# Two stacked row-and-column scans on one core: where the first pair's output and layer 1's residual are kept in DRAM, and when four groups of transfers are issued

## The chip, the cores and the metric

The kernel runs on one core of a Trainium2 chip. The time is device microseconds of the whole program on that core; the median of three runs is 4559.44 us.

## The reference, cut to what matters

`x` is (32, 48, 64, 128): batch, channel, height H, width W, all float32. Two layers run one after the other, and each adds four scans of the group-normalised input to its input. A scan step is a convolution of 5 taps over the 48 channels (width taps for the rows, height taps for the columns), with bias, plus the next line.

```python
def _conv1d(x, w, b):                      # 5 taps, padding 2
    y = jax.lax.conv_general_dilated(x, w, window_strides=(1,), padding=[(2, 2)], ...)
    return y + b[None, :, None]
def step(w, b):
    def f(carry, inp):
        nxt = inp + _conv1d(carry, w, b)
        return (nxt, nxt)
    return f
...
xs = jnp.moveaxis(x, 2, 0)
d0 = xs[0]
_, d_rest = jax.lax.scan(step(down_w, down_b), d0, xs[1:])     # down: rows 1..63
...                                                            # up: rows back to 0
_, r_rest = jax.lax.scan(step(right_w, right_b), r0, ws[1:])   # right: columns 1..127
...
_, l_rest = jax.lax.scan(step(left_w, left_b), l0, R[Ww - 2::-1])
...
x = x + _L0_conv_ref(_gn(x), L0_...)       # _gn: 16 groups of 3 channels, per image
x = x + _L1_conv_ref(_gn(x), L1_...)
return x
```

Every step needs the one before it, so the chain of steps is the spine of the program: 63 down, 63 up, 127 right and 127 left for each image and layer.

## The kernel before, in words

**Tiling.** The 32 images are four groups of 8 (`GB`). A row phase scans one group down and up: 126 steps. A column phase scans a pair of groups right and left: 254 steps. A step is nine products of 128x128 by 128 columns on TensorE (two instructions each) into three PSUM tiles, and three additions on VectorE (`step`, L630 to L657). The partitions hold (8 neighbouring rows or columns e) x (48 channels) in three tiles of 128 (`NG`, index o); `PIECES` lists the ten stretches of partitions that belong to one e, and every transfer that touches this layout is issued piece by piece.

**Phases.** `PHASES` is a fixed order of 12: rows of layer 0 groups 0 and 1, columns of layer 0 pair 0, rows 0/2, rows 1/0, rows 0/3, columns 0 pair 1, rows 1/1, 1/2, 1/3, columns 1 pair 0 (k = 10), columns 1 pair 1 (k = 11). Between a row phase and the column phase the data goes through DRAM (`ups`) to change layout; the input with rows in order is kept in `xin`, and layer 0's result, which layer 1 takes in, in `mid`. Both are lists of one DRAM tensor for each group (`kept`, `source`).

**Buffers.** SBUF has three slots. A row phase uses two of them. A column phase has four quarters of its columns and three slots: quarters 0 and 3 share one, so quarter 0 is written to DRAM (`spill_unit`) after the right scan has passed it and brought back before the left scan ends. A quarter has six units (o, group) of 128 x 2048 numbers, 1 MB. Four more 1 MB tiles (`stage`) hold residuals and results on their way; in layer 1 two are `nats` (residual in) and two are `perms` (result out).

**Output of a layer 1 column phase.** For each of 24 units, in the order of quarters 3, 2, 1, 0: `load_residual` on ScalarE's queue, `add_permuted` on GpSimd (eight additions that also reorder), and `store_result`, which writes runs of 32 numbers (128 bytes) into `out`, half on SyncE's queue and half on ScalarE's. Units of quarter 2 free the slot into which the next phase's quarter 0 is loaded, units of quarter 1 that for its quarter 1, and units of quarter 0 that for its quarter 2.

**Order.** Nothing is scheduled by the machine. `at(t, fn, ...)` puts a piece of work into `agenda` at a step number t; before each scan step the work due by then is emitted, and `in_order` ties each engine's instructions to that order. An engine's queue, SyncE's and ScalarE's DMA queues too, therefore runs strictly in this order, and each waits for what its next entry needs. The step number is a place in the order, not a time at which something is held back. `plan_rows` (L753), `plan_cols` (L790), `plan_input` (L733) and `first_group` (L912) fill the agenda.

**Places that the change touches.** `move_rows` (L500) moves rows between DRAM and the slots, in runs of 128 bytes. `plan_rows` stores the last rows of the up scan in the blocks 8 to 15, 2 to 7 and 0 to 1 when the column phase of the same pair follows (`follows`, true for k = 2 and k = 6). The column phase then loads quarter 0 of the second group in stretches on ScalarE's queue:

```python
at(t0 - 13 + i, load_unit, k, 0, i, 2, NH, 0, E8, other)     # rows 16 to 63
at(t0 - 6 + i / n, load_unit, k, 0, i, 1, 2, 0, E8, other)   # rows 8 to 15
at(t0 - 1.5, load_unit, k, 0, i, 0, 1, E8 // 4, E8, other)   # rows 2 to 7
at(t0, load_unit, k, 0, i, 0, 1, 0, E8 // 4, other)          # rows 0 and 1
```

In `first_group`, group 0 is loaded, permuted on GpSimd, written to `xin` and read back in the scan's layout by `move_rows`, then scaled on ScalarE by `scale_rows`; the last eight rows (56 to 63) are read back at step 20 of the agenda (L1040), behind the first loads of group 1 (`take_in`, L1036), and rows 48 to 63 are scaled at step 34 (L1042).

Of the kernel before, what the change touches and what calls it, by code (L numbers as in the profile page):

```python
# [30 lines left out]
C = 48  # L34
# [57 lines left out]
def kernel(  # L92
# [22 lines left out]
    NBN = H * W // (2 * BN)  # L115
    CHANNEL = H * W * GB
    PAD = 1024
    assert N == FULL and SLOT == NG * HALF * N and SLOT == 6 * UNIT

    cpool = ctx.enter_context(tc.tile_pool(name="cpool", bufs=1))  # L120
# [26 lines left out]
    def kept(name):  # L147

        return [
            dram.tile([C, CHANNEL + PAD], F32, tag=f"{name}{g}", name=f"{name}{g}")[:, 0:CHANNEL]  # L150
            for g in range(NGRP)
        ]

    source = [kept("xin"), kept("mid")]
    ups = [kept("upa"), kept("upb")]
    taps = [
        [dram.tile([C, TAPS, C], F32, tag=f"taps{i}{j}", name=f"taps{i}{j}") for j in range(3)]
# [3 lines left out]
        dram.tile([2 * NG, FULL, UNIT], F32, tag=f"spill{i}", name=f"spill{i}")  # L161
        for i in range(4)
    ]

    def by_row(t, e, h0, h1):


        t = t.rearrange("c (i q a e n) -> e a c i q n", i=E8, q=NQ, a=NH, e=E8)[e, h0 // E8]
        return t[:, h0 % E8 : h0 % E8 + h1 - h0].rearrange("c i q n -> c (i q) n")

    def lines(t, h0, h1):

        t = t.rearrange("c (i q a n) -> a c i q n", i=E8, q=NQ, a=NH)[h0 // E8]
        return t[:, h0 % E8 : h0 % E8 + h1 - h0].rearrange("c i q n -> c (i q) n")

    def by_col(t, e, j):


        return t.rearrange("c (i q n) -> i q c n", i=E8, q=NQ)[e, j]

    def dma(dst, src, queue=None):
        (queue or nc.sync).dma_start(dst, src)
# [21 lines left out]
    def pieces(o):  # L204
        return [(e, c0, c1, p0) for e, c0, c1, g, p0 in PIECES if g == o]
# [278 lines left out]
    def put_out(g, h, perm, stride):  # L484

        n = perm.shape[-1] // (W * GB)
        for s in range(2):
            dma(
                lines(source[0][g], h + s * stride, h + s * stride + n),
                perm[SIDES[s]].rearrange("p (m n) -> p m n", n=LINE),  # L490
            )

# [7 lines left out]
    def move_rows(k, h0, h1, to_dram):  # L500

        _, layer, g = PHASES[k]
        view = row_views(k)[h0 // HALF]
        t = (ups if to_dram else source)[layer][g]
        for h in range(h0, h1, E8):
            end = min(h1, h + E8)
            for o in range(NG):
                for e, c0, c1, p0 in pieces(o):
                    here = view[p0 : p0 + c1 - c0, o, h % HALF : h % HALF + end - h]
                    here = here.rearrange("p h (q n) -> p (h q) n", q=NQ)  # L510
                    there = by_row(t, e, h, end)[c0:c1]
                    if to_dram:
                        dma(there, here)
                    else:
                        dma(here, there)

    def scale_rows(k, h0, h1):
        _, layer, g = PHASES[k]
# [22 lines left out]
    def quarter(k, j):  # L541
        return slot[slots(k)[j % 3]].rearrange("p (o s n) -> p s o n", s=2, o=NG)
# [24 lines left out]

    HH = NH // 2  # L570

    def load_residual(k, j, i, nat):
        _, layer, pair = PHASES[k]
        if layer == 0:
            o, half = UNITS[i]
            t = source[0][2 * pair + half]
            for e, c0, c1, p0 in pieces(o):
                dma(nat[p0 : p0 + c1 - c0], by_col(t, e, j)[c0:c1])
            return
        o, r = divmod(i, 2)  # L580
        view = nat.rearrange("p (s n) -> p s n", s=2)
        part = slice(r * HH * LINE, (r + 1) * HH * LINE)
        for e, c0, c1, p0 in pieces(o):
            for s in range(2):
                dma(
                    view[p0 : p0 + c1 - c0, s],
                    by_col(source[1][2 * pair + s], e, j)[c0:c1, part],
                    nc.scalar,
                )

    def add_residual(k, j, i, nat):
        o, half = UNITS[i]
# [3 lines left out]
    def keep_result(k, j, i):  # L596
        _, layer, pair = PHASES[k]
        o, half = UNITS[i]
        for e, c0, c1, p0 in pieces(o):
            dma(  # L600
                by_col(source[1][2 * pair + half], e, j)[c0:c1],
                quarter(k, j)[p0 : p0 + c1 - c0, half, o],
            )

    def add_permuted(k, j, i, nat, perm, engines):
# [9 lines left out]
                    dst[:, a, s], res[:, a, s], inp[:, a, s], ALU.add  # L615
                )

    def store_result(k, j, i, perm):
        pair = PHASES[k][2]
        o, r = divmod(i, 2)  # L620
        both = out[2 * pair * GB : 2 * (pair + 1) * GB]
        dst = both.rearrange("b c (a e) w -> e a c b w", e=E8)[..., j * WQ : (j + 1) * WQ]
        src = perm.rearrange("p (a b n) -> p a b n", a=HH, b=2 * GB)
        for a in range(HH):
            for e, c0, c1, p0 in pieces(o):
                to = nc.sync if a < HH // 2 else nc.scalar
                dma(dst[e, r * HH + a, c0:c1], src[p0 : p0 + c1 - c0, a], to)


# [90 lines left out]
    def at(t, fn, *args):  # L720
        agenda.append((t, len(agenda), fn, args))
# [68 lines left out]
    def plan_cols(k, t0, prev):  # L790
        _, layer, pair = PHASES[k]
        n = 2 * NG
        after = prev == "cols"
        for i in range(n):
            if follows(k) and UNITS[i][1] == 1:
                other = nc.scalar
                at(t0 - 13 + i, load_unit, k, 0, i, 2, NH, 0, E8, other)
                at(t0 - 6 + i / n, load_unit, k, 0, i, 1, 2, 0, E8, other)
                at(t0 - 1.5, load_unit, k, 0, i, 0, 1, E8 // 4, E8, other)
                at(t0, load_unit, k, 0, i, 0, 1, 0, E8 // 4, other)  # L800
                at(t0 + 1.5, load_unit, k, 1, i)
            else:
                early = 30 if after else 46 if k == 2 else 70
                at(t0 - early + 2 * i, load_unit, k, 0, i)
                at(t0 + (3 if after else 0.5 if follows(k) else -24 + 2 * i), load_unit, k, 1, i)
            at(t0 + (38 if after else 8) + 2 * i, load_unit, k, 2, i)
            at(t0 + 33 + 2 * i, spill_unit, k, i, False)
            at(t0 + 50 + 2 * i, load_unit, k, 3, i)
        final = k == len(PHASES) - 1
        left = t0 + W - 1  # L810
        end = left + W - 1
        for i in range(n):
            at(left + 64 + 2 * i, spill_unit, k, i, True)
        units = []
        for n_done, j in enumerate((3, 2, 1, 0)):
            every = 4.5
            if j == 0 and PHASES[k + 1 if not final else k][0] == "rows":
                every = 7
            units += [(left + 34 + 32 * n_done + every * i, j, i) for i in range(n)]
        stats = None  # L820
        if layer == 0:
            stats = ResultStatsV(f"r{2 * pair}"), ResultStatsA(f"r{2 * pair + 1}")
        tiles = [stage[:, i] for i in range(4)]
        nats, perms = (tiles, None) if layer == 0 else (tiles[0:2], tiles[2:4])
        ahead = len(nats)

        for u, (t, j, i) in enumerate(units):
            nat = nats[u % ahead]
            o, half = UNITS[i]
            if u < ahead:  # L830
                at(left + 16, load_residual, k, j, i, nat)
            elif not (final and j == 0):
                at(units[u - ahead][0] + (3 if layer == 0 else 4.9), load_residual, k, j, i, nat)
            if layer == 0:
                at(t, add_residual, k, j, i, nat)
                at(t + 4, keep_result, k, j, i)
                unit = quarter(k, j)[:, half, o]
                if half == 0:
                    for b in range(GB):
                        at(t + 5 + b, stats[0].take, j, o, unit, b)  # L840
                else:
                    at(t + 1, stats[1].take, j, o, unit)
            elif not (final and j == 0):
                perm = perms[u % 2]
                at(t, add_permuted, k, j, i, nat, perm, [nc.gpsimd])
                at(t + 5, store_result, k, j, i, perm)
        if layer == 0:
            t = units[-1][0] + 14
            g = 2 * pair
            spread(t, scaling(f"r{g}", 1, g, stats[0], r_masks), 1)  # L850
            spread(t + 20, scaling(f"r{g + 1}", 1, g + 1, stats[1], r_masks), 1)
        if final:
            at(left + 97, last_loads, k)
            at(end + 4, last_results, k)
# [57 lines left out]
    def first_group():  # L912
# [119 lines left out]
        scale_rows(0, 24, 32)  # L1032
        move_rows(0, 32, 48, False)
        scale_rows(0, 32, 40)
        move_rows(0, 48, 56, False)
        take_in(1, 0, nats1[0])  # L1036

    in_order(first_group)
    at(starts[0] + 10, scale_rows, 0, 40, 48)
    at(starts[0] + 20, move_rows, 0, 56, 64, False)  # L1040
    at(starts[0] + 22, take_in, 1, 16, nats1[1])
    at(starts[0] + 34, scale_rows, 0, 48, 64)  # L1042

    agenda.sort(key=lambda a: a[:2])
    done = 0
# [65 lines left out]
```

## Time and profile before

| | |
|---|---|
| three runs | 4550.92, 4559.44, 4564.35 us |
| profiled execution | span 4546.3 us, mean granted TensorE clock 0.964 |
| TensorE busy | 4163.2 us, 92% of the span |
| DMA | 661.55 MB, mean 146 GB/s; 2010816 of 2124132 packets are under 512 bytes |
| chain that ended last | TensorE 77%, DMA 15% |

TensorE is the engine that matters: the scans are a chain. What can be won lies in the places where it stands still, before its first step, after its last, and between. The DMA row says that nearly all packets are small: `xin`, `ups` and `out` are reached in runs of 128 bytes when the layout changes, whereas quarters, spills and residuals move in runs of 4 or 8 KB. In the tables by stretch, the last two columns are the busy share of the 16 DMA engines and what they moved; a share of 1.0 or over is a stretch in which they are full.

### The profile page before, as it was taken

The numbers are of one execution on the slowest core, as the hardware profiler recorded it, in microseconds if no ns is written. First come the engines' busy times: TensorE is split into PE (matmuls) and PEld (weight loads), VectorE is DVE, ScalarE is ACT, GpSimd is POOL, SyncE is SP. The second block draws the span as 40 slices with busy tenths as digits, with TensorE's granted clock in tenths as the row PEclk, the third lists the DMA queues.
The fourth block names the chain that finished last, engine by engine and source line by source line (L and its number), as shares of the span: only waits on it lengthen the run. The fifth ranks groups of instructions, "written<-read, shape, count | busy, mean of one in ns | idle before, by whom it ended". The sixth has DMA issues, their size and how long they took to land.

```text
span 4546.3 us, 90798 instructions
## 1 busy us (share of the span) xinstructions
PE 4163.2 (92%) x36632; PEld 4132.1 (91%) x36632; DVE 2180.9 (48%) x6594; ACT 1183.5 (26%) x2334; POOL 907.7 (20%) x943
## 2 busy tenths in 40 slices
PE   4889997999999999979999999999999997879990
PEld 2889997999999999979999999999999997869990
DVE  5445443446654444434456654444444443334441
ACT  1553302426776445000025944330000000000000
POOL 4441001314412020000024300000000155500554
PEclk9999998999999999989999999999999998889995
DMA  9989789857989999489038989394790099970799
GB/s 176 176 163 157 114 146 194 202 105 237 221 163 160 162 150 155 75 151 199 6 89 241 204 148 150 48 143 84 117 207 12 18 195 181 200 188 1 148 172 163
DMA packets 2124132, 661.55 MB, mean 146 GB/s; under 512 B 2010816, under 2 KB 2063808, under 8 KB 2092224
## 3 DMA queue, kind: packets, MB, share of 16 engines
q1 hardware_dynamic: 1901312, 573.92, 66.5%
q10 hardware_dynamic: 222400, 81.83, 9.5%
q8 instruction: 288, 4.72, 0.5%
q14 instruction: 132, 1.08, 0.1%
HBM read 378.70 MB, written 277.11 MB: 144 GB/s over the span
## 4 chain that ended last, share of the span: by engine, by line
PE 77%; DMA 15%; SPq 2%; ACT 2%; POOL 1%; ACTq 1%; issue 1%; DVE 0%; POOLq 0%; DVEq 0%
DMA out<-arena 6%; PE step_01r L641 6%; PE step_00r L641 6%; PE step_10r L641 6%; PE step_00l L641 6%; PE step_01l L641 6%; DMA arena<-mid 4%; PE step_11r L641 3%; PE step_00u L641 3%; PE step_11d L641 3%; PE step_02u L641 3%; PE step_11u L641 3%; PE step_10u L641 3%; PE step_13u L641 3%; PE step_13d L641 3%; PE step_12u L641 3%
## 5 line engine op out<-in xcount | busy, mean ns | idle before, releaser
L525 ACT ACTIVATE arena<-arena,offset,scale 128x256 f32<-128x256 f32 (+2 forms) x840 | 594.7, 802 | 449.3 <-DVE arena L650 151.8
L614 POOL TENSOR_TENSOR arena<-arena 128x256 f32<-128x256 f32 x336 | 349.1, 1082 | 973.1 <-DVE arena L650 717.6
L482 POOL COPY arena<-arena 112x256 f32<-112x256 f32 x458 | 270.9, 648 | 764.1 <-DMA arena<-in_x 469.0
L880 ACT COPY arena<-arena 128x256 f32<-128x256 f32 x18 | 10.5, 644 | 1470.9 <-DMA out<-arena 1467.9
L594 POOL TENSOR_TENSOR arena<-arena 128x2048 f32<-128x2048 f32 x48 | 217.7, 4562 | 835.7 <-PE step_01l L641 543.5
L641 PE MATMUL step_11r<-arena,wright 128*128 128x128 f32 x2286 | 267.3, 281 | 85.7 <-DVE arena L650 37.6
L641 PEld LDWEIGHTS step_11r<-arena,wright 128*128 128x128 f32 x2286 | 265.4, 198 | 87.5 <-DVE arena L650 55.8
L416 ACT ACTIVATE junk<-arena 128x256 f32<-128x256 f32 x192 | 129.6, 675 | 699.2 <-POOL arena L594 693.1
L641 PE MATMUL step_01r<-arena,wright 128*128 128x128 f32 x2286 | 258.8, 277 | 29.3 <-DMA arena<-upa 29.3
L641 PEld LDWEIGHTS step_01r<-arena,wright 128*128 128x128 f32 x2286 | 258.4, 194 | 29.7 <-issue 29.5
L641 PE MATMUL step_00r<-arena,wright 128*128 128x128 f32 x2286 | 257.4, 276 | 29.2 <-DMA arena<-upa 29.2
L641 PEld LDWEIGHTS step_00r<-arena,wright 128*128 128x128 f32 x2286 | 257.0, 193 | 29.6 <-issue 29.4
L641 PE MATMUL step_00l<-arena,wleft 128*128 128x128 f32 x2286 | 256.3, 275 | 0.0
L641 PE MATMUL step_10r<-arena,wright 128*128 128x128 f32 x2286 | 256.0, 275 | 0.0
L641 PEld LDWEIGHTS step_10r<-arena,wright 128*128 128x128 f32 x2286 | 255.7, 192 | 0.3
L641 PEld LDWEIGHTS step_00l<-arena,wleft 128*128 128x128 f32 x2286 | 255.7, 192 | 0.0
L641 PE MATMUL step_01l<-arena,wleft 128*128 128x128 f32 x2286 | 255.4, 275 | 0.0
L641 PE MATMUL step_10l<-arena,wleft 128*128 128x128 f32 x2286 | 255.4, 275 | 0.0
L641 PE MATMUL step_11l<-arena,wleft 128*128 128x128 f32 x2286 | 255.4, 275 | 0.0
L641 PEld LDWEIGHTS step_01l<-arena,wleft 128*128 128x128 f32 x2286 | 255.3, 192 | 0.0
L641 PEld LDWEIGHTS step_10l<-arena,wleft 128*128 128x128 f32 x2286 | 255.3, 192 | 0.0
L641 PEld LDWEIGHTS step_11l<-arena,wleft 128*128 128x128 f32 x2286 | 255.3, 192 | 0.0
(173 smaller groups left out, 6989.0 us busy)
## 6 DMA issues: line engine op xcount, KB each, us to landing
xin<-arena SPq DMA_DIRECT2D x96, 384.0 KB, 5.5
arena<-xin SPq DMA_DIRECT2D x96, 384.0 KB, 8.5
mid<-arena SPq DMA_DIRECT2D x96, 384.0 KB, 8.0
arena<-mid SPq DMA_DIRECT2D x192, 192.0 KB, 4.4
upb<-arena SPq DMA_DIRECT2D x192, 192.0 KB, 3.9
arena<-mid ACTq DMA_DIRECT2D x192, 192.0 KB, 4.7
arena<-upb SPq DMA_DIRECT2D x96, 384.0 KB, 10.7
arena<-xin SPq DMA_DIRECT2D x186, 192.0 KB, 4.3
```

Of the source, the lines that this page charges most:

```text
L416: nc.scalar.activation(junk[:, 0:n], view[:, b], AF.Identity, accum_out=self.sum[:, i, j : j + 1])
L482: copy(dst[:, r, q], src[:, r0 + r, q])
L525: nc.scalar.activation(args[0], args[0], AF.Identity, bias=args[2], scale=args[1])
L594: nc.gpsimd.tensor_tensor(unit, unit, nat, ALU.add)
L614: engines[(2 * a + s) % len(engines)].tensor_tensor(dst[:, a, s], res[:, a, s], inp[:, a, s], ALU.add)
L641: nc.tensor.matmul(part(whole(ps[o]), -s), weights[:, i, FULL * (o - NG * s - i + 1) : FULL * (o - NG * s - i + 2)], part(src(i), s), star ...
L880: copy(dst[:, a, s], src[:, a, s])
```

## The change

1. `mid` becomes two tensors, one for each pair of groups, with the halves of a unit's rows (r) outside and the two groups (s) inside. So `load_residual` of layer 1 is one DMA of 8 KB runs for each piece in place of two of 4 KB runs, while `keep_result` (layer 0) writes 4 KB runs in place of 8 KB runs. `move_rows` of layer 1 reads the same 128-byte runs from other addresses.
2. In phase 10 the 12 units of quarters 1 and 0 are no longer stored into `out` from SBUF. Each is written as it stands, one DMA of 1 MB in 8 KB runs on SyncE's queue, into a DRAM tensor `held[n]`; later, behind all loads of phase 11's quarters in that queue's order, `store_result` moves it from `held[n]` into `out`, DRAM to DRAM, all on SyncE's queue.
3. At the two places where a column phase follows its own row phase, rows 32 to 63 of the second group's quarter 0 are loaded 18 steps earlier than rows 16 to 31.
4. In `first_group` rows 56 to 63 are read back with rows 48 to 55, ahead of the first loads of group 1, and rows 48 to 63 are scaled in two parts at steps 26 and 32 in place of one at step 34.

```diff
+    HH = NH // 2
-    source = [kept("xin"), kept("mid")]
+    xin = kept("xin")
+    mid = [
+        dram.tile([C, 2 * CHANNEL + PAD], F32, tag=f"mid{i}", name=f"mid{i}")[:, 0 : 2 * CHANNEL]
+        for i in range(NGRP // 2)
+    ]
...
+    held = [dram.tile([FULL, UNIT], F32, tag=f"held{i}", name=f"held{i}") for i in range(4 * NG)]
...
+    def pair_row(t, s, e, h0, h1):
+        t = t.rearrange("c (i q r s a e n) -> s r a e c i q n", i=E8, q=NQ, r=2, s=2, a=HH, e=E8)
+        r, a = divmod(h0 // E8, HH)
+        t = t[s, r, a, e][:, h0 % E8 : h0 % E8 + h1 - h0]
+        return t.rearrange("c i q n -> c (i q) n")
+    def pair_col(t, e, j):
+        return t.rearrange("c (i q r n) -> i q c r n", i=E8, q=NQ, r=2)[e, j]
...
         o, r = divmod(i, 2)
-        view = nat.rearrange("p (s n) -> p s n", s=2)
-        part = slice(r * HH * LINE, (r + 1) * HH * LINE)
         for e, c0, c1, p0 in pieces(o):
-            for s in range(2):
-                dma(
-                    view[p0 : p0 + c1 - c0, s],
-                    by_col(source[1][2 * pair + s], e, j)[c0:c1, part],
-                    nc.scalar,
-                )
+            dma(nat[p0 : p0 + c1 - c0], pair_col(mid[pair], e, j)[c0:c1, r], nc.scalar)
...
+            n = UNIT // 2
             dma(
-                by_col(source[1][2 * pair + half], e, j)[c0:c1],
-                quarter(k, j)[p0 : p0 + c1 - c0, half, o],
+                pair_col(mid[pair], e, j)[c0:c1, :, half * n : (half + 1) * n],
+                quarter(k, j)[p0 : p0 + c1 - c0, half, o].rearrange("p (r n) -> p r n", n=n),
             )
...
-    def store_result(k, j, i, perm):
+    def store_result(k, j, i, perm, queues=(nc.sync, nc.scalar)):
...
-                to = nc.sync if a < HH // 2 else nc.scalar
+                to = queues[a * len(queues) // HH]
...
-                at(t0 - 13 + i, load_unit, k, 0, i, 2, NH, 0, E8, other)
+                at(t0 - 31 + i, load_unit, k, 0, i, 4, NH, 0, E8, other)
+                at(t0 - 13 + i, load_unit, k, 0, i, 2, 4, 0, E8, other)
...
-                at(t + 5, store_result, k, j, i, perm)
+                if final or j > 1:
+                    at(t + 5, store_result, k, j, i, perm)
+                else:
+                    n = 2 * NG * (1 - j) + i
+                    at(t + 5, dma, held[n], perm)
+                    at(end + 104 + 4.5 * n, store_result, k, j, i, held[n], [nc.sync])
...
-        move_rows(0, 48, 56, False)
+        move_rows(0, 48, 64, False)
         take_in(1, 0, nats1[0])
...
-    at(starts[0] + 20, move_rows, 0, 56, 64, False)
     at(starts[0] + 22, take_in, 1, 16, nats1[1])
-    at(starts[0] + 34, scale_rows, 0, 48, 64)
+    at(starts[0] + 26, scale_rows, 0, 48, 56)
+    at(starts[0] + 32, scale_rows, 0, 56, 64)
```

More of the change, by code (lines that the diff above doesn't have):

```diff
@@ L488, in put_out @@
             dma(
-                lines(source[0][g], h + s * stride, h + s * stride + n),
+                lines(xin[g], h + s * stride, h + s * stride + n),
                 perm[SIDES[s]].rearrange("p (m n) -> p m n", n=LINE),
@@ L503, in move_rows @@
         view = row_views(k)[h0 // HALF]
-        t = (ups if to_dram else source)[layer][g]
+        t = ups[layer][g] if to_dram else mid[g // 2] if layer else xin[g]
         for h in range(h0, h1, E8):
@@ L510, in move_rows @@
                     here = here.rearrange("p h (q n) -> p (h q) n", q=NQ)
-                    there = by_row(t, e, h, end)[c0:c1]
                     if to_dram:
-                        dma(there, here)
+                        dma(by_row(t, e, h, end)[c0:c1], here)
+                    elif layer:
+                        dma(here, pair_row(t, g % 2, e, h, end)[c0:c1])
                     else:
-                        dma(here, there)
+                        dma(here, by_row(t, e, h, end)[c0:c1])
     def scale_rows(k, h0, h1):
@@ L566, in spill_unit @@
             dma(there, here)
-    HH = NH // 2
     def load_residual(k, j, i, nat):
@@ L575, in load_residual @@
             o, half = UNITS[i]
-            t = source[0][2 * pair + half]
+            t = xin[2 * pair + half]
             for e, c0, c1, p0 in pieces(o):
```

## The prediction

> **What bounds the kernel now.** I read the page first: TensorE is busy for 4163.2 of 4546.3 us, so at most some 380 us can be won, all of it where TensorE stands still. Next, who TensorE waited for (total, times, longest, in us):
>
> ```profile
> PE step_11r L641 <- DVE arena L650: 37.6, 4, 18.8
> PE step_00d L641 <- DVE arena L650: 34.8, 3, 19.2
> PE step_11r L641 <- DMA arena<-mid: 32.8, 2, 16.9
> PE step_01r L641 <- DMA arena<-upa: 29.3, 1, 29.3
> PE step_00r L641 <- DMA arena<-upa: 29.2, 1, 29.2
> PE step_11r L641 <- DMA arena<-upb: 15.3, 1, 15.3
> ```
>
> The three rows of step_11r are the start of phase 11: 85.7 us together. The two of about 29 us are the starts of phases 2 and 6, one 19.2 us stop of step_00d is phase 0. The names after the arrow are the last arrival, not the cause; the chain of waits gives that. For phase 11's last stop (start, length, what):
>
> ```profile
> 3977.87 12.26 DMA out<-arena
> ...
> 3991.21 7.51 DMA out<-arena
> ...
> 4017.48 9.53 DMA arena<-upb
> ...
> 4027.03 10.85 DMA arena<-upb
> ...
> 4038.41 1.65 PE step_11r L641 x6
> ```
>
> Phase 11's quarter 2 (upb) comes late because phase 10's output is late. Whether the DMA engines are full there, and at which rate, the table by stretch tells (span, TensorE, its loads, VectorE, ScalarE, GpSimd, clock, DMA share and GB/s):
>
> ```profile
> 400.00:450.00 50.00, 47.66 (x424) 47.30 (x423) 22.29 (x70) 23.22 (x31) 0.00 (x0) 1.00 1.01 157
> 1100.00:1150.00 50.00, 50.00 (x450) 50.00 (x450) 34.02 (x94) 39.75 (x99) 20.69 (x5) 1.00 1.01 299
> 3800.00:3840.00 40.00, 16.01 (x137) 15.53 (x135) 7.08 (x23) 0.00 (x0) 17.11 (x17) 0.73 1.10 178
> 3980.00:4000.00 20.00, 20.00 (x182) 20.00 (x181) 9.49 (x31) 0.00 (x0) 0.00 (x0) 1.00 0.98 265
> 4060.00:4220.00 160.00, 160.00 (x1434) 159.93 (x1433) 76.53 (x239) 0.00 (x0) 0.00 (x0) 1.00 0.02 5
> 4230.00:4426.00 196.00, 192.43 (x1724) 192.24 (x1722) 94.38 (x289) 0.00 (x0) 116.01 (x112) 1.00 0.92 180
> 4426.00:4546.00 120.00, 0.00 (x0) 0.00 (x0) 20.84 (x17) 10.47 (x18) 49.36 (x50) 0.50 1.03 164
> ```
>
> The first row is row moves in 128-byte runs alone: full at 157 GB/s. Runs of 8 KB reach 299 (loads) and 265 (loads beside spills). The stops of phase 11 lie in a full stretch at a mixed 178; 160 us of empty DMA follow at once; then phase 11's own output fills the engines to the end, 120 us past the last step. So a unit of 1 MB (1.049 million bytes) costs 6.7 us stored in short runs and 4.0 in long ones. These are my prices.
>
> The 19.2 us stop of phase 0, in the chain:
>
> ```profile
> 204.38 10.20 DMA arena<-in_x
> ...
> 225.54 5.35 DMA arena<-xin
> ...
> 231.00 14.78 ACT arena L525 x20
> ```
>
> Rows 56 to 63 are read back behind group 1's first loads, and the scaling waits for them.
>
> **What the Trainium skill says.** "DMA: Bandwidth & Descriptors", section "Why small descriptors are slow (HBM only)": each packet carries a fixed overhead. The trace agrees: 157 against 265 to 299. Same page, section "Issuing engines are not separate DMA queues": SyncE's and ScalarE's transfers share the same 16 engines, so a second queue saves only issue time; hence I count bytes, not queues. Same page, section "Latency and other measured facts": row pitches of 4 MiB in DRAM halved a copy, 512 KiB hardly did, and a padding of 4 KiB restored it. The pitch of `mid` goes from 260 to 516 KiB with that padding kept, so I expect no loss; no run here shows it yet. On the rate from DRAM to DRAM no page bears.
>
> **The change part by part.** All against the profiled span, 4546.3 us; the three runs lie around it, median 4559.44.
>
> *Phase 10 into 11.* From 3780 (quarter 2's output done, quarter 0 of phase 11 begins to load) to 4038 are 258 us. In it move three quarters of upb and one spill, 25.2 MB in long runs; 11 residual units, 11.5 MB; 12 units of output and the rest of one, 13 MB in short runs. At my prices 36.7/265 + 13/157 = 138 + 83 = 221 us. So 37 us more than the engines' price pass, in which one queue or the other waited. After: 49.3 MB in long runs and 1 MB in short ones, 186 + 7 = 193 us: 28 us less. Of the 37 us some goes too. ScalarE's queue loses the 80 stores of these quarters and half of its residual loads (76 of 152 in this window, median issue 0.38 us, 29 us), so a residual no longer stands behind a store; SyncE's queue loses 80 stores for 12 writes, so the quarter loads come up sooner, and GpSimd (8.6 us of work for a unit, some 15 us from unit to unit here) waits less. None to all: 0 to 37, I take 18. Fewer residual DMAs in quarters 3 and 2 bring quarter 2's end forward by 0 to 10, I take 6. Sum 52 us, bounds 28 and 75. What a new write adds: GpSimd's next but one unit waits for a whole 1 MB to land (spill writes: median 11.3 us for a row that both directions share) in place of two halves; two tiles in turn hide that at 8.6 us a unit, or it stays in the 37. What stays queued behind the held writes on SyncE: phase 11's quarters, spills, then the moves into `out`.
>
> *The moves into `out`.* 160 DMAs on SyncE's queue, issue at 0.3 to 0.5 us: 50 to 80 us. Their data cost 12 x 6.7 = 80 us if the DRAM source is no slower than SBUF. They start when quarter 3's loads are issued (4054 before, some 4000 after) and SyncE is wanted next for phase 11's first stores (4231 before, some 4175 after). 175 us of nearly empty DMA hide them: nothing. The price from DRAM is not in the trace except in 30 tiny copies of the taps (median 2.0 us to landing, no slower than others); lower bound 6.7 us a unit, upper bound twice that, a read and a write in turn: 160 us, still hidden.
>
> *The tail.* Phase 11's output moves the same bytes, with half of the residual DMAs (80 in place of 160). It is full at 0.92 to 1.03, so from nothing to 0.8 us a unit, 20 us; I take 8.
>
> *Starts of phases 2 and 6.* Of 2304 KB loaded at step -13, 1536 KB move 18 steps (36 us) forward: 1.57/265 = 6 us of DMA fewer in the stretch where the last stores of the up scan must land. Those stores (3 x 10 DMAs), their landing, and the last load stay. ScalarE waits in its queue for the earlier rows; it computes nothing in those stretches (its row is 0.0 from 550 to 700 and from 1800 to 2050), so nothing stands behind. At phase 2 the engines are full around 590 to 640, where the loads now go, and this may give part back. 0 to 12 each; I take 7 and 7: 14 us.
>
> *Phase 0.* The stop of 19.2 us goes: ten loads (14 us of SyncE's issue, 211 to 225) pass ahead of group 1's first 16 loads, which come some 10 us later, while its next 16 come no later; rows 48 to 55 are scaled at 204 to 217, 56 to 63 by 230, and TensorE wants them at 227 and 243. But phase 1 waits for group 1: it stopped 2.1 and 7.4 us for rows that come off a SyncE queue which is full from 363 to 500 (157 GB/s), and that begins when GpSimd's permuting of group 1 ends at 362. That chain gets shorter only where its stores no longer stand behind a load: GpSimd goes on at some 247 in place of 252.8. So of 19.2 us won, 13 are lost again in phase 1: 6 us; bounds 0 and 19.
>
> *Writing `mid` in 4 KB runs.* Same bytes, hidden under the scans, but at the start of phase 3 (one stop of 4.6 us, DMA share 0.95) it can cost 0 to 5; I take 2.
>
> Sum: 52 + 8 + 14 + 6 - 2 = 78 us. Span 4468; on the median 4559.4 - 78, about 4480 us.
>
> **The rivals.**
> *The bytes alone count* (12%): the waits of phase 11 only change their names, because quarter 2 and the spill still stand behind the last held write; the other parts come to nothing. 28 - 5 = 23 us: 4536. For it: the full shares. Against it: 37 us that bytes don't explain.
> *All stops go* (10%): 85.7 + 24 + 19 + 20 = 149 us: 4410. Against it: the sum of bytes above leaves phase 11 some 30 us short.
> *Slower: the moves from DRAM into `out` block SyncE's queue* (7%). The place is that queue between quarter 3's loads and phase 11's first stores; the price is p us a unit against the 175 us there. All above 175/12 = 14.6 us a unit is paid at the end, since the tail is full. At 21 us a unit (50 GB/s) the whole gain of 78 is gone; at 26 us (40 GB/s) 312 - 175 - 78 = 59 us slower, 4618. For it: the price is not in the trace. Against it: it would need three times the price of the same runs from SBUF.
> *It does not do what it says*: the held moves could run in the full stretch. The order in SyncE's queue puts them behind quarter 3's loads, so no.
>
> **How the numbers follow.** My sum has 68%: 4480. All its bounds on one side at once would give 4421 or 4536 (75 + 20 + 24 + 19 = 138, or 28 - 5 = 23); most of its chance lies between 4435 and 4530. Up to 4545 the range also takes in the first rival with the spread of the runs (4551 to 4564), and down to 4420 a part of the second; so some 80% lie from 4420 to 4545. The remaining 3% fall about no change. A measurement here can tell 0.3% (14 us) from no change. Faster by more: 68 + 12 + 10 = 90%; within: 3%; slower: 7%.
>
> **What would show it.** Right: step_11r's waits fall from 85.7 to some 35 us, with the last stop before quarter 2; the DMA share from 4010 to 4110 is high in place of 0.02; the 29 us stops become some 22; step_00d's 19.2 goes while step_01d's waits grow from 9.7 to some 20; the tail stays at 110 to 120 us. Wrong: held moves still running at phase 11's first stores, step_11r's waits near 60, or a new wait in the row phases of layer 1 that read the new `mid`.

## The result, and the profile after

The changed kernel takes 4585.93 us (median of 4, 4579.25 to 4590.56) against 4559.63 us beside it (4 runs): the ratio is 1.0059, 95% interval 1.0037 to 1.0081. That is some 27 us slower, where 78 us less were forecast. Its profiled execution has a span of 4588.5 us, 42.2 more than the one shown of before. The ratio is the measure; the span says where. TensorE itself is busy for 4166.6 us, against 4163.2 before: nearly all of the difference is time in which it stands still.

Who TensorE waited for in the changed kernel (total, times, longest, us):

```profile
PE step_11r L656 <- DVE arena L665: 46.6, 5, 16.4
PE step_00r L656 <- DMA arena<-upa: 27.1, 1, 27.1
PE step_01r L656 <- DMA arena<-upa: 24.3, 1, 24.3
PE step_00d L656 <- DVE arena L665: 22.0, 3, 11.3
PE step_11l L656 <- DVE arena L665: 21.3, 3, 15.3
PE step_11r L656 <- DMA arena<-upb: 16.9, 1, 16.9
PE step_11r L656 <- DMA arena<-mid: 14.1, 1, 14.1
PE step_00u L656 <- DVE arena L665: 9.6, 1, 9.6
```

Phase 11's right scan still stops for 46.6 + 16.9 + 14.1 = 77.6 us (85.7 before). The row of step_11l is new: its left scan now stops for 21.3 us. The tail, the time from the last product to the end, is 157.4 us long (123.9 before). So the loss lies behind phase 11's right scan, where the forecast saw nothing but idle DMA and a tail of 110 to 120 us. The table by stretch of the changed kernel (span, TensorE, its loads, VectorE, ScalarE, GpSimd, clock, DMA share, GB/s) shows what happens there:

```profile
4060.00:4110.00 50.00, 50.00 (x449) 49.93 (x448) 23.99 (x75) 0.00 (x0) 0.00 (x0) 1.00 0.67 106
4120.00:4210.00 90.00, 90.00 (x808) 90.00 (x807) 42.76 (x135) 0.00 (x0) 0.00 (x0) 1.00 0.00 1
4224.00:4288.00 64.00, 64.00 (x576) 64.00 (x575) 30.68 (x96) 0.00 (x0) 5.04 (x5) 1.00 0.81 128
```

The moves into `out` begin at 4042.9, run at 106 GB/s and stop behind the 86th, at 4113. For 110 us next to nothing moves (the second row). The other 74 of the 160 run from 4224 to 4288, in the middle of phase 11's own output. The waits of SyncE's queue from 4040 to 4300 have one large row:

```profile
SPq L204 <- DMA arena<-mid: 111.3, 2, 110.1
```

SyncE waited 110.1 us at one DMA, for a residual load (arena<-mid) that ScalarE issued. The chain of waits tells what that load waited for:

```profile
4150.45 61.42 PE step_11l L656 x550
...
4213.41 7.33 POOL arena L629 x7
...
4220.76 0.31 ACTq L204
...
4221.11 5.22 DMA arena<-mid
...
4226.35 0.55 SPq L204
```

The left scan reaches the first columns that may be put out; GpSimd adds the first unit; this frees a buffer; ScalarE issues the residual load of the third unit into it, piece by piece; and when the first piece lands, SyncE goes on with a move of `held[6]`, the 87th, which has no data in common with it. (The chain passes by the second piece, for which the 89th move waits in the same way.) GpSimd's timeline gives the price of what followed (start, length, ..., idle before it):

```profile
4212.38 16.67 POOL L629 TENSOR_TENSOR arena<-arena 128x256 f32<-128x256 f32 x16 [247.84 <-DVE arena L665]
4293.91 16.63 POOL L629 TENSOR_TENSOR arena<-arena 128x256 f32<-128x256 f32 x16 [64.87 <-DMA out<-arena]
```

After its first two units GpSimd stood still for 64.9 us, since SyncE's half of their stores stood behind 74 moves. Before, the same third unit followed without a gap of over 1 us (4247.0).

Why should a move wait for another queue's load? In the program as built, every DMA of SyncE and ScalarE raises one of eight completion counters. They are handed out in turn over both queues in one common order, and a DMA that is given a counter first waits until its last user has landed. The 87th move got the counter of that first piece, and this is the only counter that it waits for. The trace agrees: the piece was issued at 4220.76 and landed at 4223.82, and the move began at 4223.84. So much is read off; the experiments test it.

### The profile page after: what moved, and what is told of

It is laid out like the page before. It is cut to its first block, busy times and chain, and to the rows that moved or that the text cites. A ratio compares the mean times of both kernels' runs of the same rounds, so it can differ in the third digit from the quotient of the medians.

```text
span 4588.5 us, 90518 instructions
## 1 busy us (share of the span) xinstructions
PE 4166.6 (91%) x36632; PEld 4134.6 (90%) x36632; DVE 2183.2 (48%) x6594; ACT 1189.9 (26%) x2358; POOL 907.4 (20%) x943
## 4 chain that ended last, share of the span: by engine, by line
PE 78%; DMA 13%; SPq 3%; ACT 2%; POOL 1%; issue 1%; DVE 1%; ACTq 1%; POOLq 0%; DVEq 0%
PE step_00r L656 6%; PE step_01r L656 6%; PE step_10r L656 6%; PE step_00l L656 6%; PE step_01l L656 6%; DMA out<-arena 4%; PE step_11r L656 4%; PE step_10l L656 3%; SPq L204 3%; PE step_11u L656 3%; PE step_10u L656 3%; PE step_00u L656 3%; PE step_13u L656 3%; PE step_13d L656 3%; PE step_12u L656 3%; PE step_12d L656 3%
## 5 line engine op out<-in xcount | busy, mean ns | idle before, releaser
L656 PE MATMUL step_11r<-arena,wright 128*128 128x128 f32 x2286 | 266.0, 281 | 77.6 <-DVE arena L665 46.6
L656 PE MATMUL step_11l<-arena,wleft 128*128 128x128 f32 x2286 | 259.5, 277 | 21.3 <-DVE arena L665 21.3
```

The source lines that it names most:

```text
L656: nc.tensor.matmul(part(whole(ps[o]), -s), weights[:, i, FULL * (o - NG * s - i + 1) : FULL * (o - NG * s - i + 2)], part(src(i), s), star ...
```

## The experiments

Below, "pairs" is part 1 of the change (the paired `mid`) and "held" part 2. Four kernels take the change apart, eight follow the question of the queue and what was left behind it. All times are ratios to the kernel before on the same chip; stops of the two scans and tails (us) are those of one profiled execution each. How far those scatter: the changed kernel, and the same with its moves elsewhere or left out, run the same work up to quarter 3, and step_11r stops for 77.6, 64.9 and 67.7 us in them. So the argument rests on the ratios; the stops only say where to look.

| run | ratio, 95% interval | step_11r | step_11l | tail |
|---|---|---|---|---|
| before | 1 | 85.7 | 0 | 123.9 |
| the change | 1.0059 (1.0037 to 1.0081) | 77.6 | 21.3 | 157.4 |
| early loads alone (parts 3, 4) | 0.9982 (0.9974 to 0.9990) | 85.6 | 0 | 125.5 |
| without held (1, 3, 4) | 1.0002 (0.9993 to 1.0012) | 88.7 | 0 | 128.5 |
| held alone (2) | 1.0030 (1.0018 to 1.0042) | 65.1 | 9.2 | 148.0 |
| without pairs (2, 3, 4) | 1.0005 (0.9996 to 1.0014) | 63.7 | 9.2 | 147.1 |
| without pairs, moves on ScalarE | 0.9917 (0.9904 to 0.9930) | 63.6 | 0 | 123.9 |
| all parts, moves on ScalarE | 0.9940 (0.9928 to 0.9952) | 64.9 | 0 | 127.5 |
| all parts, moves left out | 0.9950 (0.9937 to 0.9963) | 67.7 | 0 | 130.4 |
| without held, residuals in 4 KB runs | 0.9969 (0.9957 to 0.9981) | 85.6 | 0 | 122.4 |
| without pairs, moves on both queues | 0.9932 (0.9919 to 0.9946) | 59.2 | 0 | 125.5 |
| without pairs, moves and quarter 0's held writes on ScalarE | 0.9892 (0.9879 to 0.9906) | 52.6 | 0 | 123.1 |
| all parts, moves on ScalarE, 4 KB runs | 0.9917 (0.9904 to 0.9929) | 54.7 | 0 | 123.5 |
| the same, and quarter 0's held writes on ScalarE | 0.9892 (0.9875 to 0.9908) | 54.5 | 0 | 125.8 |

### The parts one by one

Without `held` (the changed kernel with this branch of `plan_cols` undone):

```diff
-                if final or j > 1:
-                    at(t + 5, store_result, k, j, i, perm)
-                else:
-                    n = 2 * NG * (1 - j) + i
-                    at(t + 5, dma, held[n], perm)
-                    at(end + 104 + 4.5 * n, store_result, k, j, i, held[n], [nc.sync])
+                at(t + 5, store_result, k, j, i, perm)
```

> The changed kernel without its part 2: all output of phase 10 goes straight from SBUF into out, as before; the paired mid, the earlier loads and the front stay. Theory A (the loss is the moves from held into out, of which the 87th waits some 110 us for a completion that it shares with ScalarE's queue, so that 74 of them run in the middle of phase 11's output): the stops of step_11l (21 us) and the longer tail (157 us in place of 120) go, the gains at the starts of phases 2, 6 and 11 stay (7 us): 4545 to 4556 us. Theory B (the paired mid makes the residual loads slower, about 20% a byte in the packet records): phase 10's output and the tail stay slow, 4570 to 4590 us.

Measured 4556.90 us, ratio 1.0002: 1 us above A's range, 13 us below B's. The left scan's stops go and the tail is 29 us shorter.

The opposite, the kernel before with the `held` branch alone:

> The kernel before with part 2 alone: half of phase 10's output by way of held. Theory A: moves still end up behind the start of phase 11's output, so some 20 to 40 us of tail and of left-scan stops come against some 10 us won in phase 11: 4570 to 4590 us. Theory B: without the paired mid the held output wins in phase 11 and loses nothing after: 4520 to 4550 us.

Measured 4566.12 us, ratio 1.0030: slower by itself as A has it, though 4 us below A's range. In its profile step_11r stops 20 us less, but the left scan's stops and the tail give back more than that.

The change without the paired `mid` (part 1), and the two groups of early loads alone (parts 3 and 4 in the kernel before):

> The changed kernel without its part 1: mid as one tensor for each group, residual of layer 1 in two DMAs of 4 KB runs. By the built program the first move that shares its completion with a transfer of phase 11 is then the 110th, not the 87th. Theory A: 51 moves late in place of 74, so about two thirds of the loss: 4560 to 4575 us. Theory B: no slow residual loads, all gains kept: 4520 to 4545 us.

> The kernel before with parts 3 and 4 alone (the earlier loads at phases 2 and 6, rows 56 to 63 ahead of group 1). Both theories: some 7 to 12 us off, as the changed kernel's phase 11 starts 7 us earlier, and nothing lost after: 4545 to 4553 us. If it is slower than the kernel before, the loss sits in these parts and both theories fall.

The first measured 4555.50 us (1.0005), which lies between the ranges, below A by 4 us and above B by 10; the second 4546.24 us (0.9982), as expected by both. The early loads are worth 0.18%, 8 us. `held` on top of them costs 1.0005/0.9982, 0.23%, 10 us, and the pairs a further 1.0059/1.0005, 0.54%, 25 us. Without pairs the same wait is there, with fewer moves left behind it: SyncE's moves stop behind the 109th, as was read off the built program before the run, and the waits of its queue have

```profile
SPq L184 <- DMA out<-arena: 135.0, 20, 115.1
```

This time the releaser is a store of phase 11's output from ScalarE's queue. With pairs ScalarE issues half as many residual loads, the common order counts otherwise, and the sharing begins with the 87th move: 74 late moves in place of 51. The wait's cost thus hangs on the number of DMAs on the other queue. That is why the pairs seem to cost so much here: without any move in the way they cost 0.20% (1.0002 against 0.9982).

### Is it the queue, or the bytes?

The moves were given to ScalarE, which is idle from 4010 to 4210, ahead of its residual loads for phase 11. One tiny copy of a column that the scan writes at step 92 holds them back until quarter 3's loads are done. First without pairs, then with:

```diff
-                    at(end + 104 + 4.5 * n, store_result, k, j, i, held[n], [nc.sync])
+                    at(end + 92.6 + 4 * n, store_result, k, j, i, held[n], [nc.scalar])
...
         if final:
+            at(t0 + 92.5, hold_back, k)
...
+    def hold_back(k):
+        n = (92 % E8) * KQ * GB + (92 // E8 % KQ) * GB
+        nc.scalar.copy(junk[:, 0:1], slot[slots(k)[2]][:, n : n + 1])
```

> The change without the paired mid, but with the 160 moves into out issued by ScalarE in place of SyncE, behind one tiny ScalarE copy of a column that phase 11's right scan writes at step 92, and ahead of phase 11's residual loads. No move then stands behind phase 11's output, and no store of phase 11 behind a move. Theory A (the moves themselves are cheap; what costs is that the last 51 of them wait on SyncE for a transfer of phase 11's output, and stand in front of its stores): moves done by about 4180, no stops of step_11l, phase 11's right stops about 64, a tail of 122 to 130 after the last product: 4515 to 4535. Theory B (the moves cost their bytes wherever they lie, in contention with phase 11's output or its loads): 4545 to 4560, as without the edit.

> The changed kernel whole, paired mid included, with the moves issued by ScalarE as in the run above. A: the 21 us of stops of step_11l go and the tail falls by some 25 to 35: 4528 to 4545. B: within 10 us of the changed kernel, 4575 to 4595. The distance from the run without pairs is the price of the paired mid: some 10 to 25.

Measured 4514.40 us (0.9917) and 4524.99 us (0.9940). Against the same kernels with the moves on SyncE that is 0.9917/1.0005, 0.9% or 40 us, and 0.9940/1.0059, 1.2% or 54 us. The left scan does not stop, and the tails are 123.9 and 127.5. Theory A stands in both; the times are 1 and 3 us below its ranges. The moves now run without a break (engine queue, operation, count: shortest/median/longest ns, first and last start), from the group of the tile `held` in the run with pairs, and, for comparison, in the changed kernel:

```profile
L204 ACTq DMA_DIRECT2D out<-held x160: 576/660/1664, 4060.8 to 4178.6; - x160
```

```profile
L204 SPq DMA_DIRECT2D out<-held x160: 549/647/5290, 4042.9 to 4287.9; - x160
L204 SPq DMA_DIRECT2D held<-arena x12: 319/320/338, 3802.6 to 3964.6; - x12
```

And the changed kernel with the line of the moves taken out, so that 12 units of `out` are not written:

```diff
-                    at(end + 104 + 4.5 * n, store_result, k, j, i, held[n], [nc.sync])
```

> The changed kernel with the 160 moves left out, so that 12 of the 48 units of out (quarters 1 and 0 of the first pair) are not written. It gives the whole cost of the moves. A: the left scan's stops go and the tail is that of the kernel before or shorter: 4525 to 4540, and within 8 us of the run with the moves on ScalarE. B (moves innocent; the paired mid slows phase 11's output): 4570 to 4590. If the moves cost bytes too, this run is over 10 us faster than the one with the moves on ScalarE.

Measured 4528.22 us, ratio 0.9950, no better than with all moves on ScalarE (0.9940; the intervals overlap). So 12.6 million bytes moved from DRAM to DRAM in that stretch cost nothing that can be measured; "hidden" was right for the bytes and wrong for the place in the queue. These runs take away the late start of the moves and their place ahead of phase 11's stores together; moves that stay on SyncE's queue without a shared counter were not tried, so how the loss divides between the two stays open (the 74 late moves alone take 48 us to issue). The sharing of counters itself is still there: in the run with pairs SyncE's queue waits 159.4 us for one of ScalarE's moves. It costs nothing there, since SyncE's next store, at 4195.9, then still has to wait for GpSimd's first unit.

### What a move costs

The moves divided between both queues, without pairs:

```diff
-                    at(end + 92.6 + 4 * n, store_result, k, j, i, held[n], [nc.scalar])
+                    at(end + 92.6 + 4 * n, store_result, k, j, i, held[n])
```

> The run with the moves on ScalarE and without the paired mid, with the moves divided between SyncE and ScalarE (half each, as the ordinary stores are). If the issue of a DMA from DRAM to DRAM (0.65 us each) is what makes them slow, they take about half of the time, some 55 to 65 us in place of about 105, and the DMA share while they run goes from 0.6 to about 1; the total stays within 8 us of the run on ScalarE alone, 4510 to 4524, since they lie in an idle stretch either way. If the DMA engines are slow in reading DRAM and writing 128-byte runs, they take over 90 us as before.

Measured 4516.56 us, 0.9932 (0.9917 on ScalarE alone: no gain, as expected). One queue, and then two, by stretch:

```profile
4100.00:4160.00 60.00, 60.00 (x539) 60.00 (x539) 28.77 (x90) 0.00 (x0) 0.00 (x0) 1.00 0.70 111
```

```profile
4100.00:4140.00 40.00, 40.00 (x360) 40.00 (x359) 19.00 (x61) 0.00 (x0) 0.00 (x0) 1.00 1.14 154
```

With one queue the DMA engines are busy for 0.70 of the time at 111 GB/s; with two they are full at 154 GB/s, about the 157 of short runs from SBUF. So DRAM as a source is not slower; the issue is, with a median of 0.65 us a DMA on one queue, for pieces of 96, 64 and 32 KB alike, and 0.55 on each of two, against 0.32 for SyncE's writes from SBUF. From 4060 to the last landing the moves took 90 us, in place of 119 on one queue: a gain, but not the 55 to 65 expected, because from a share of 0.70 only 1.0 can be reached. SyncE's first few moves had gone out at 4026, and there its queue stood for 35.9 us, until ScalarE's first moves landed: the shared counters again.

### What the pairs cost

Without `held`, each residual load out of the paired tensor in two DMAs:

```diff
         for e, c0, c1, p0 in pieces(o):
-            dma(nat[p0 : p0 + c1 - c0], pair_col(mid[pair], e, j)[c0:c1, r], nc.scalar)
+            n = UNIT // 2
+            for s in range(2):
+                half = slice(s * n, (s + 1) * n)
+                t = pair_col(mid[pair], e, j)[c0:c1, r, half]
+                dma(nat[p0 : p0 + c1 - c0, half], t, nc.scalar)
```

> The change without held, but with each residual load of layer 1 issued as two DMAs of 4 KB runs out of the paired tensor in place of one of 8 KB runs: run length and number of DMAs as before, row pitch 516 KiB as in the change. If the length of the runs makes the paired loads slow: 4543 to 4550, like the run with the early loads alone (4546), and a 4 KB packet takes some 265 ns. If the row pitch or the place in DRAM does: 4553 to 4560, like the run without held (4557), and a 4 KB packet takes 310 ns or more.

Measured 4537.15 us, 6 us below the range for the length of the runs, with the packet time expected there. The ratio is 0.9969, against 1.0002 with 8 KB runs and 0.9982 with `mid` by groups. The packets of ScalarE's queue between 3620 and 3680, worked out from the packet records of the trace:

```
kernel                                     bytes   packets   mean ns   ns per KB
before                                      4096      1024       261          65
without held (8 KB runs, pitch 516 KiB)     8192       566       615          77
the same in 4 KB runs, pitch 516 KiB        4096      1087       259          65
the change                                  8192       558       639          80
```

So the pitch is innocent, and the longer packet is the dearer one here, by some 20% for each byte. Why, the runs don't tell (nor how much of the 0.33% comes from the packets: the edit also doubles the number of these DMAs, and so changes which DMAs share a counter); 8 KB packets of other tensors are not slow as such (402 ns, 50 ns per KB, on SyncE's queue in the same stretch of the run with 4 KB runs).

All parts with moves on ScalarE and residuals in 4 KB runs (both diffs above):

> All parts of the change, with the moves on ScalarE and with each residual load in two DMAs of 4 KB runs out of the paired tensor. If one DMA of 8 KB runs is the whole cost of the pairs: as the run without pairs, 4508 to 4520; if the place in DRAM has a cost when held is there too: 4520 to 4530.

Measured 4513.39 us, 0.9917: what the run without pairs gave, and in the first range. Pairing the groups has no measurable use here and, in short runs, no cost.

### What is left of phase 11's stops

The moves no longer in the way, `held` without pairs brings 0.9917/0.9982, 0.65% or 30 us, where 46 were forecast (52, less 6 for the residual DMAs), and step_11r still stops for 63.6 us. In the changed kernel GpSimd stands still before the third unit of quarter 0:

```profile
3881.71 8.35 POOL L629 TENSOR_TENSOR arena<-arena 128x256 f32<-128x256 f32 x8 [2.83 <-DMA arena<-mid]
3929.68 16.60 POOL L629 TENSOR_TENSOR arena<-arena 128x256 f32<-128x256 f32 x16 [39.62 <-DMA held<-arena]
```

The write of quarter 0's first unit to `held[6]` stands in SyncE's queue behind phase 11's quarter 1 loads, which came up at step 3 and wait for quarter 1's units. Without pairs, with ScalarE's moves, that idle time is 28.2 us. The edit gives quarter 0's held writes to ScalarE:

```diff
-                    at(t + 5, dma, held[n], perm)
+                    at(t + 5, dma, held[n], perm, None if j else nc.scalar)
```

> The run with the moves on ScalarE and without the paired mid, with the six held writes of quarter 0 issued by ScalarE, so that they no longer stand behind phase 11's quarter 1 loads in SyncE's queue. Theory A (a queue wait, not the bytes, keeps phase 11's right stops at 64 us): GpSimd's idle time of about 28 us ahead of unit 20 goes, quarter 2 is free some 15 to 25 us earlier, the stops fall to 40 to 52: 4492 to 4508. Theory B (the loads of both queues together are slow, and these bytes set the end): the stops stay at 60 to 68, 4510 to 4520.

Measured 4500.27 us, ratio 0.9892. In GpSimd's timeline two short idle times, 6.48 and 7.24 us, have taken the place of the 28.2:

```profile
3880.05 8.33 POOL L616 TENSOR_TENSOR arena<-arena 128x256 f32<-128x256 f32 x8 [8.87 <-DMA arena<-mid]
3894.86 8.22 POOL L616 TENSOR_TENSOR arena<-arena 128x256 f32<-128x256 f32 x8 [6.48 <-DMA arena<-mid]
3910.32 8.10 POOL L616 TENSOR_TENSOR arena<-arena 128x256 f32<-128x256 f32 x8 [7.24 <-DMA arena<-mid]
```

The stops fall to 52.6, just outside the 40 to 52 expected, and the total lies inside. The step from 0.9917 is 0.25%, 11 us. What stays is not idle DMA: in this run the engines are full in the stretches of the stops, e.g.

```profile
3800.00:3840.00 40.00, 12.71 (x84) 12.28 (x84) 4.64 (x14) 0.00 (x0) 19.05 (x19) 0.62 1.04 245
3880.00:3920.00 40.00, 22.23 (x191) 21.75 (x189) 9.69 (x31) 0.00 (x0) 24.64 (x24) 0.80 1.03 240
```

Last, all parts with all three edits:

> All parts of the change with the three edits together: moves on ScalarE, residual loads in two DMAs of 4 KB runs, and the held writes of quarter 0 on ScalarE. If the gain of the third (14 us in the run without pairs) is apart from that of the second: phase 11's right stops 40 to 48, no left stops, a tail of 120 to 126, 4494 to 4505. If the two take the same wait away: 4505 to 4516.

Measured 4511.54 us on a chip on which the kernel before took 4557.61: ratio 0.9892, as without pairs. By the time alone this is in the second range, but this chip runs the kernel before 8.5 us slower than that of the run without the third edit (4549.08). By the ratios the third edit is worth another 0.25%. Yet the intervals touch, and the profiled stops, 54.5, are those without it and not the 40 to 48 expected: what it does with pairs stays open. The best versions, this one and the kernel without pairs with moves and quarter 0's held writes on ScalarE, are 1.1% under the kernel before and 1.7% under the change.

## Why the prediction was wrong

- **The step that failed is "The moves into `out`".** "175 us of nearly empty DMA hide them: nothing" counted bytes, issue time and each queue's own order, and took the two queues as independent. The stretch was long enough (160 moves take 118 us on ScalarE) and the bytes free. But one move waited 110.1 us for ScalarE's queue, and SyncE issues in order, so phase 11's stores waited too: the prediction's own sign of being wrong, "held moves still running at phase 11's first stores". The price of this place in the queue, the wait and the late issue together, is 54 us with pairs, 40 without. The 54 are half of the 105 us between the forecast and the measurement. With the moves on ScalarE the whole change wins 27 us (0.9940), still far from 78; of the other 51, `held` takes some 18, the pairs 21 and the early parts 12, as follows. The Trainium skill ("DMA: Bandwidth & Descriptors", section "Issuing engines are not separate DMA queues") says that both queues share the 16 engines; the prediction turned that into "I count bytes, not queues". The trace agrees on the sharing (two queues moved 154 GB/s of short runs, one had moved 157), but a queue is also an order of waits.
- **The slower rival named the right place.** It said that the moves block SyncE's queue between quarter 3's loads and phase 11's first stores, but priced it by the rate from DRAM, with 14.6 us a unit as the point. 160 moves in 118 us are 9.8 us a unit; the rate did not decide, a wait did. The 0.3 to 0.5 us of issue for each move was also too low: 0.65. That no page bears on the rate from DRAM to DRAM was an oversight: the skill's measurement that it cites for the row pitch was of copies within DRAM, though of long rows.
- **Phase 10 into 11, 52 us (28 to 75): too large.** The mechanism was right (the quarters come up sooner). Of its 46 us for `held`, 28 came with pairs (0.9940/1.0002) and 30 without once the moves were out of the way, and 41 (0.9892/0.9982) with quarter 0's held writes out of SyncE's queue. "SyncE's queue loses 80 stores for 12 writes" missed that six of the 12 stand behind quarter 1's loads. That GpSimd waits less therefore held only in the last runs. The three kernels with pairs and 8 KB runs show stops of 77.6, 64.9 and 67.7 us against 85.7. The prices were misread as well: the row of 1100 to 1150, "loads" at 299 GB/s, has 20 writes of `mid` beside its loads, and in the row of 3980 to 4000 some 43 of the 265 GB/s are stores in short runs. Loads alone are slower (last section), so part of the 37 us put down to waiting queues may have been full engines; that was not tested.
- **The residual loads by pairs.** The forecast counted 6 us for them in phase 10 and 8 in the tail. They cost 0.20% (9 us, 1.0002 against 0.9982), and in the profiles the tail got 3 us longer (128.5 against 125.5). With the 2 us for the writes of `mid` taken off, a gain of 12 us was forecast; the distance is 21. Counting DMAs was the error: the bytes came more slowly. The row pitch did no harm (259 ns for a 4 KB packet, 261 before), as expected from the skill ("DMA: Bandwidth & Descriptors", section "Latency and other measured facts"). The fixed overhead of each packet, on which the section "Why small descriptors are slow (HBM only)" rests, would make 8 KB the cheaper size; here 80 against 65 ns per KB, and the measurement decides.
- **The starts of phases 2 and 6, 14 us: half.** Both stops fell, by 2.1 and 5.0 us.
- **Phase 0, 6 us: too large, and the loss comes back elsewhere than said.** The 19.2 us stop became 6.3, but TensorE now stops for 9.6 us in the up scan, for VectorE, whose timeline shows that it stood at the statistics of group 1:

```profile
313.73 1.29 DVE L351 BATCH_NORM_STATS2 bn_x<-arena 112x6 f32<-112x512 f32 x2 [9.62 <-DMA arena<-in_x]
```

  The scan's additions stand behind that instruction on VectorE. The forecast looked for the loss in phase 1, whose stops grew by some 1 us only. Phase 2 begins 3.7 us earlier, of which 2.1 are its own shorter stop: 1.6 us remain. With the two starts that makes 8.7, and parts 3 and 4 alone measured 8 us, where 20 were forecast.
- **The 4 KB writes of `mid`, 2 us:** not shown. step_02d's stop went from 4.6 to 6.6, but it is 5.1 to 9.0 in the later runs without pairs and 4.6 in one with them.

The early parts (8 us won) and `held` with its blocked queue (10 lost) about cancel; the pairs, by slow loads and by 23 more moves behind the wait, make the change slower than before.

## What to carry to other kernels

Work that is moved into an idle stretch is hidden only if its queue is idle as well: ask of every DMA in it what it may have to wait for, in the program as built and not only in its data, and what stands behind it in that queue. Where two queues share completion counters, a DMA of one can wait for the other; a trickle of late work belongs on the queue on which nothing urgent stands behind it. And a gain of a few units from fewer, longer transfers is to be checked against their rate, not counted.

## What the runs showed of the hardware that was not expected

- A DMA from DRAM to DRAM took 0.65 us to issue on either queue (medians 647 and 660 ns, and 550 and 557 where both issued), one from SBUF of 1 MB 0.32 us; with pieces of 32 to 96 KB one queue then fed the engines to 0.7 only (111 GB/s), two filled them (154 GB/s).
- 8 KB packets of the paired residual took 615 to 639 ns, 4 KB packets of the same rows 259 ns; cause open.
- Full engines moved less when all of it was loads. In the changed kernel, quarter 1's loads together with residual loads, and then both of these kinds beside a held write and spills:

```profile
3880.00:3920.00 40.00, 26.91 (x233) 26.42 (x231) 12.22 (x38) 0.00 (x0) 8.35 (x8) 0.85 1.02 174
3960.00:3980.00 20.00, 20.00 (x181) 20.00 (x180) 9.60 (x30) 0.00 (x0) 4.53 (x5) 1.00 0.93 335
```

  The engines are full in the first at 174 GB/s and move 335 in the second. It is not a matter of two queues: in the kernel before, SyncE's loads alone (upb, 8 KB runs, from 3385 to 3405) fill the engines at 175 GB/s, and its loads beside spills (2090 to 2110, 8 KB runs too) at 361. Other stretches of loads alone reach up to 240. Why, the runs don't tell. The prediction's one price of 265 for all long runs hides this.
